# The last attention block turned by TensorE, three outer products by row halves, and the rows after them in a new order

## The chip, the cores and the metric

The kernel runs on one core of one Trainium2 chip. All data is float32. The metric is the device time of one execution in microseconds (us); the median of 3 runs of the kernel before is 1077.04 us (1076.51 to 1078.44). The engines are TensorE (PE: matmuls and 128x128 transposes), VectorE (DVE), ScalarE (ACT), GpSimd (POOL) and SyncE (SP, which only issues transfers). ACT and POOL issue transfers too, each in its own order.

## What is computed

Input x is 1024 x 512. The reference, cut to what matters:

```python
# attention: 32 heads of 128, 8 key/value heads
q = (h @ w_q).reshape(B, S, 8, 4, 128); k = h @ w_k; v = h @ w_v
scores = einsum('bqhgd,bkhd->bhgqk', q, k) * 128 ** -0.5
probs = softmax(where(causal, scores, -inf))
attn = einsum('bhgqk,bkhd->bqhgd', probs, v)
attn_ref = attn.reshape(B, S, 4096) @ w_o
# FFN: a dense layer plus 8 low-rank experts of rank 16
base_out = x @ base_W.T + base_b
probs = softmax(x @ router_W.T + router_b)          # 15 logits
topk_p, topk_i = top_k(probs, 8)
w = sum over k of topk_p * onehot(expert_map[topk_i])
lora = ((x @ A) * w) @ B * 2.0
ffn_ref = base_out + lora
# the whole
x = x + layernorm(attn_ref(layernorm(x)))
x = x + layernorm(ffn_ref(layernorm(x)))
```

## The kernel before

**Rows and groups.** The 1024 rows are 8 blocks t of 128 rows. The 32 heads are 8 groups g of 4 heads, one group to a key/value head. A block of a group is worked in four score tiles j of 32 rows by 4 heads, which fill 128 partitions. Blocks are taken in units (0,1), (2,3), (4), (5), (6), (7) within each group.

**A score tile** (`scores`, from L569) goes through a chain: PE scores, DVE mask and maximum (L587), ACT exp and sum (L602), DVE reciprocal (L610), ACT product with it (L611), and DVE's 32x32 stream transpose into tile T (L618). The rest of p's last 128 columns is cleared by POOL (L567). After the last tile of a unit, `to_keys` (L628) issues 16 transfers K<-T, which bring the transposed 32x32 squares into rows of keys: on SP; in the last group also on POOL for block 6, and on SP, ACT and POOL in turn for block 7. Only then can PE form the block's weighted values (`weighted_values`, L645; `attend` does it for a unit, in that unit's K). Unit i - 2 is attended while unit i's scores are formed, mixed with "fill": other products (q, k, v of the next group, and in the last group the first three steps of the output projection). `cut` divides fill by shares among units and score tiles; `weave` mixes two lists by their cost. In the last group results go into the PSUM banks `last`.

**The output projection** is a 4096-term product. Attention output and w_o are taken in an outer scheme of seven products (Strassen-Winograd), each of which is done in an inner one of seven. Its step (n, gc, r) is outer product n, chunk gc of two heads groups (0 to 3), and row half r, or None for both. A whole step is 28 matmuls, a half step 14. To feed it, ACT copies a block's values into the pair tile `at` (two blocks side by side), DVE forms four outer sums in `pair_sums` (L671), and POOL stores the tile in memory, `attn_d` (`pair_store`, L682; seven parts, 896 KB). `fetch_a` loads a step's operand again and `sums_a` (L768) has DVE form its inner sums; `fetch_w` and `sums_w` (L785) do the same for w_o, on SP and POOL. `merge_inner` (L852) and `merge_outer` (L879) add the products up, from PSUM into `acc`, whose slices are row blocks. Even row blocks are complete after outer product n=4, odd ones after n=6.

**The FFN** for row block t: `ffn_norms` (L924: both layernorms around the first residual, in steps run one by one by `go`), `ffn_router` (L977: PE turns h, `ptx_h`, ACT copies it into hT, PE forms logits and low-rank values `pl`, then DVE, ACT and POOL form routing weights and `hw`), `ffn_out` (L1026: PE's dense products `pf`, `ptw` turns hw, ACT copies it into hwT, PE adds the experts, DVE and POOL finish with the second layernorm), and `ffn_store`. In the program order written out after L1306, steps 0 to 10 are placed by hand around the last blocks; from step 11 on `whole_step` runs each with its loads and sums (`begin_step`, L1354, which forms the sums of step k + 2 ahead). FIRST = 28 is the first half step: outer product 6 is done by halves, r = 0 first (rows 1 and 3, called c and d), then r = 1 (rows 5 and 7, e and f). Rows 0, 2, 4 and 6 of the FFN are woven with these eight half steps; `NORMS` says in which half step which row advances by a norm's step. Rows c to f follow in the tail.

Engines execute their instructions in program order, so a waiting instruction holds up all that stands behind it on its engine.

Of the kernel before, what the change touches and what calls it, by code (L numbers as in the profile page):

```python
# [15 lines left out]
P = 128  # L16
# [6 lines left out]
def kernel(  # L23
# [82 lines left out]
    for k in range(NCH):  # L106
        halves = 2 if k == NCH - 1 else 1
        names = [f"attn_d{k}_{r}" for r in range(halves)]
        shape = [7, GC, P, NT * P // halves]
        attn_d.append([dram.tile(shape, F32, tag=name, name=name) for name in names])  # L110
        wo_d.append(dram.tile([4, GC, P, 2 * hn], F32, tag=f"wo_d{k}", name=f"wo_d{k}"))

# [439 lines left out]
    score_tile = {}  # L552
# [16 lines left out]
    def scores(g, t, j):  # L569

# [36 lines left out]

        def rescale():
            rec = small.tile([P, 1], F32, tag="rec", name=f"rec_{name}")
            keep(nc.vector.reciprocal(rec, total))  # L610
            keep(nc.scalar.mul(p[:, :n], p[:, :n], rec))  # L611
# [14 lines left out]
        score_tile["rescale"], score_tile["finish"] = rescale, finish  # L626

    def to_keys(g, u):  # L628
        size = sum(t + 1 for t in u) * NSUB * P
        src = turned.pop((g, u))[:, :size].rearrange("p (b n) -> p b n", b=NSUB)  # L630
        w = turn_tile("K", g, u)
        dst = w[:, :size].rearrange("p (h n) -> p h n", h=R)
        for t in u:
            keyed[g, t] = turn_view(w, t)
        by = [nc.sync]
        if g == G - 1 and u[0] >= 6:
            by += [nc.gpsimd] if u[0] == 6 else [nc.scalar, nc.gpsimd]
        for h in range(R):
            for b in range(NSUB):
                load(dst[ts(b, SQ), h], src[ts(h, SQ), b], by[(h * NSUB + b) % len(by)])  # L640

    pair_tiles = {}
    last_banks = []

    def weighted_values(g, t):  # L645

        def finish(po):
            if t % 2 == 0:
                pair_tiles[g, t // 2] = act.tile(
                    [P, 7, 2, P], F32, tag="at", name=f"at_{g}_{t // 2}"  # L650
                )
            o = pair_tiles[g, t // 2][:, 2 * (t % 2) : 2 * (t % 2) + 2]
            pinned(nc.scalar.copy(o.rearrange("p a h q -> p (a h q)"), po))
            keyed.pop((g, t))
# [16 lines left out]
    def pair_sums(m):  # L671
        g, u = divmod(m, NT // 2)
        a11, a12, a21, a22, s1, s2, s4 = (pair_tiles[g, u][:, n] for n in range(7))
# [8 lines left out]
    def pair_store(m):  # L682
        g, u = divmod(m, NT // 2)
        at = pair_tiles.pop((g, u)).rearrange("p n h q -> p n (h q)")
# [14 lines left out]
    steps += [(1, 0, None), (1, 1, None), (0, NCH - 1, 1), (1, 2, None), (1, 3, None)]  # L699
    steps += [(n, gc, None) for n in range(2, 6) for gc in range(NCH)]  # L700
    FIRST = len(steps)
    steps += [(6, gc, r) for r in range(2) for gc in range(NCH)]
    HALF = 7 * GC * P
    A_TAGS = ((turn, "T0"), (turn, "K0"), (turn, "K1"), (big, "xnT"), (big, "tx"))
    a_parts, w_parts, ring = {}, {}, {"a": 0}

    def load_a(part, c, by):
        n, gc, r = steps[c]
        size = NT // 2 * P
# [12 lines left out]
    def early_a(c):  # L722

        a, y = divmod((0, 1, 2, 3, 0, 1, 2, 0, 0, 3)[c], 2)
# [19 lines left out]
    def fetch_w(n, gc, by=nc.sync):  # L744
# [3 lines left out]
        places = ("v skv", "wq", "qT", "wo wot", "qT", "wq", "qT", "qT", "wq", "wo wot", "qT", "qT")  # L748
        tags = places[k if (k := n * NCH + gc) < 8 else 8 + k % NCH].split()
        pools = {"qT": (act, 2), "v": (act, 3)}  # L750
        tiles = []
        for tag in tags:
            pool, bufs = pools.get(tag, (wp, 1))
            shape = [P, 2 // len(tags), half]
            tiles.append(pool.tile(shape, F32, tag=tag, name=f"o{tag}_{name}", bufs=bufs))
        w = [tile[:, y] for tile in tiles for y in range(2 // len(tags))]
# [11 lines left out]
    def sums_a(c):  # L768
        a, r = a_parts[c], steps[c][2]
        nr = 2 if r is None else 1  # L770
# [14 lines left out]
    def sums_w(n, gc):  # L785
# [3 lines left out]
        sums = w[1].rearrange("p (n g q) -> p n g q", n=4, g=GC)  # L789
        t1, t2, t3, t4 = (sums[:, y] for y in range(4))  # L790
# [3 lines left out]

    def fetch(c):
        n, gc, r = steps[c]
        fetch_a(c)
        for k in range(1 if r is None else 2):
            if r in (None, 0):
                fetch_w(n, gc + k)  # L800

    def step_sums(c):
        n, gc, r = steps[c]
        sums_a(c)
        if r in (None, 0):
            sums_w(n, gc)
# [45 lines left out]
    def merge_inner(n, r=None):  # L852
        nr = 2 if r is None else 1
        if (n, r) == (0, 1):
            whole = merged[0]
        else:
            rows = 2 if n == 0 else nr
            whole = act.tile([P, 2 * rows, hn], F32, tag="p", name=f"om_{n}_{r}", bufs=3)
        to = whole.rearrange("p (r e) (c q) -> p r e c q", e=2, c=2)
        if n == 0:  # L860
            to = to[:, r : r + 1]
# [17 lines left out]
    def merge_outer(n, r=None):  # L879
# [5 lines left out]
        new = merged[n]  # L885
# [60 lines left out]
    def prepare_ffn():  # L946
        ra = act.tile([P, KC, NR + ER], F32, tag="v", name="ra_sb", bufs=3)
# [17 lines left out]
    mexp = const.tile([P, E, NR], F32, tag="mexp", name="mexp")  # L965

    def prepare_map():
        emap_f = const.tile([P, NR], F32, tag="emap_f", name="emap_f")
        keep(nc.vector.tensor_copy(emap_f, late["map"]))
        for n in range(E):  # L970
            keep(
                nc.vector.tensor_scalar(
                    mexp[:, n, :], emap_f, float(n), SCALING, ALU.is_equal, ALU.mult
# [3 lines left out]
    def ffn_router(t):  # L977
# [19 lines left out]
        def route(pl, ex, total):  # L997
# [13 lines left out]
            keep(nc.vector.tensor_tensor(ws, mexp, every, ALU.mult))  # L1011
            w = small.tile([P, E], F32, tag="w", name=f"w_{t}")
            keep(nc.vector.tensor_reduce(w, ws, AX.X, ALU.add))
            hw = state["hw", t] = wp.tile([P, E, RANK], F32, tag="wk", name=f"hw_{t}")
# [241 lines left out]
    LAST_A_SUMS = ((1, 3), (3, 0), (4, 3), (7, 1))  # L1256
# [4 lines left out]
    for i, (g, u) in enumerate(order):  # L1261
        if u[0] == 0:
            if g < G - 1:
                fill = cut(group_fill(g), FILL if g else FIRST_FILL)
            else:
                first = sum((step_products(k) for k in range(3)), [])
                fill = cut(group_fill(g), (1, 1)) + cut(first, (5, 1.5, 1.3, 1.2))
# [6 lines left out]
        else:  # L1274
            ahead, mine = cut(mine, (1, 1) if u[0] == 5 else (3, 7))
# [3 lines left out]
        for (t, n), part in zip(tiles, parts):  # L1279
            loads(g, t, n)  # L1280
            scores(g, t, n)
            pool_work(g, t, n)
            run(part)
# [23 lines left out]
    finish_scores()  # L1307
# [3 lines left out]
    held.update({t: [] for t in range(NT)})  # L1311
    acc_all = turn.tile([P, NT // 2, 2, H], F32, tag="T1", name="acc")
    acc = [acc_all[:, t // 2, t % 2, :] for t in range(NT)]
    run(attend(NU - 2))
    pair_sums(N // 2 - 2)
    pair_store(N // 2 - 2)
    sums_a(4)
    sums_a(5)
    fetch_a(8)
    sums_w(1, 0)  # L1320
    one_step(3)
    one_step(4)
    sums_a(6)
# [3 lines left out]
    run(attend(NU - 1))  # L1327
    sums_a(8)
    sums_w(1, 1)
    fetch_a(10)  # L1330
    one_step(6)
    pair_sums(N // 2 - 1)
    pair_store(N // 2 - 1)
    fetch_w(1, 2)
    fetch_a(9)
    fetch_a(11)
    one_step(7)
    sums_a(9)
    sums_w(1, 2)
    fetch_w(1, 3)  # L1340
    one_step(8)
    sums_a(10)
    fetch_w(2, 0)
    one_step(9)
    fetch_a(12)
# [3 lines left out]
    fetch_a(13)  # L1349
    fetch_w(2, 1)  # L1350
    sums_a(12)
    sums_w(2, 0)

    def begin_step(k):  # L1354
        if k + 3 < FIRST:
            fetch(k + 3)
        if k >= FIRST - 2 and (k - FIRST) % 2 == 0 and k + 2 < len(steps):
            fetch(k + 2)
        if k + 2 < FIRST:
            step_sums(k + 2)  # L1360
        if k >= FIRST - 1 and k + 1 < len(steps):
            step_sums(k + 1)

    evens = (0, 2, 4, 6)
    NORMS = {-4: (0, 2), -3: (0, 4, 6), -2: (2, 0, 4), -1: (0, 2, 6, 4), 0: (2, 6, 4), 1: (6,)}
    NORMS.update({4: (c, d), 5: (c, d), 6: (c, d), 7: (c, d)})

    def hook(*rows):
        return [(0, lambda: go(*rows))]
# [4 lines left out]
    routers = {t: ffn_router(t) for t in range(NT)}  # L1374
    outs = {t: ffn_out(t) for t in (*evens, c, d, e)}

    def whole_step(k):
        j = k - FIRST
        work = later(lambda: begin_step(k))
        if j in NORMS:  # L1380
            work += hook(*NORMS[j])
        work += step_products(k)
        n, gc, r = steps[k]
        if gc == NCH - 1:
            work += later(lambda: (merge_inner(n, r), merge_outer(n, r)))
        if k == 11:
            work += later(prepare_ffn)
        if k == 14:
            work += later(prepare_map)
        if j == -6:  # L1390
            work += later(lambda: [reload_x(t) for t in evens])
        if j == -5:
            work += later(lambda: [ffn_norms(t, nc.scalar, nc.gpsimd) for t in evens])
        if j == 3:
            work += later(lambda: (reload_x(c, d), ffn_norms(c), ffn_norms(d)))
        return work

    for k in range(11, FIRST):
        run(whole_step(k))

    rows = []
    rows += routers[0][0]
    for n, t in enumerate(evens):
        turn_next = routers[evens[n + 1]][0] if n < 3 else []
        rows += routers[t][1] + hook(t) + outs[t][0] + turn_next + outs[t][2]
        if n:
            rows += hook(evens[n - 1]) + later(lambda t=evens[n - 1]: ffn_store(t))
        rows += outs[t][1] + outs[t][3] + hook(t)
    run(weave(sum((whole_step(k) for k in range(FIRST, len(steps))), []), rows))

    reload_x(e, f)
    ffn_norms(e)
    ffn_norms(f)
    out_c, out_d, out_e = (outs[t] for t in (c, d, e))
    turn_c, prod_c = routers[c]
    turn_d, prod_d = routers[d]
    turn_e, prod_e = routers[e]
    turn_f, prod_f = routers[f]
    go(e, f)
    run(turn_c + prod_c)  # L1420
    go(e, c, evens[-1])
    ffn_store(evens[-1])
    run(out_c[0] + turn_d + out_c[2])
    go(f, e)
    run(prod_d)
    go(f, d, e)
    run(out_c[1] + out_d[0])
    go(f)
    run(out_c[3])
    go(c)  # L1430
    run(out_d[2] + turn_e + out_d[1])
    go(c)
    run(out_d[3] + prod_e)
    go(d, e)
    run(out_e[0] + out_e[2][:1] + turn_f + out_e[2][1:] + prod_f)
# [50 lines left out]
```

## Time and profile before

The profiled execution took 1076.29 us, its span (first to last instruction) is 1074.5 us; the median of the three runs is 1077.04.

| | busy us | share of span | instructions |
|---|---|---|---|
| PE | 1028.9 | 96% | 4722 |
| DVE | 747.9 | 70% | 1786 |
| ACT | 476.4 | 44% | 948 |
| POOL | 366.6 | 34% | 609 |

Stretches of the last third (busy us of each engine, the clock that TensorE was granted as a share of full speed, and the DMA engines' busy share):

| from to, us | what runs | PE | DVE | POOL | PE clock | DMA |
|---|---|---|---|---|---|---|
| 700 to 750 | last group, blocks 0 to 4 | 45.85 | 38.11 | 24.46 | 0.97 | 0.75 |
| 750 to 800 | last group, blocks 5 to 7 | 42.77 | 33.28 | 17.97 | 0.94 | 0.78 |
| 820 to 840 | the very last block's values | 14.42 | 8.57 | 3.69 | 0.83 | 0.89 |
| 840 to 900 | outer products, whole steps | 60.00 | 46.57 | 37.97 | 1.00 | 0.91 |
| 900 to 960 | the same | 60.00 | 49.75 | 38.05 | 1.00 | 0.74 |
| 960 to 980 | product 6 begins | 13.79 | 14.43 | 14.77 | 0.95 | 0.49 |
| 980 to 1000 | product 6 and FFN rows | 20.00 | 11.02 | 4.54 | 0.88 | 0.01 |
| 1000 to 1020 | the same | 16.67 | 14.14 | 2.91 | 0.97 | 0.28 |
| 1020 to 1034 | its end | 13.71 | 8.49 | 4.23 | 0.79 | 0.11 |
| 1034 to 1075 | the tail: rows c to f | 29.48 | 28.06 | 8.96 | 0.94 | 0.12 |

Rows of the profile read as: line of the program, engine, operation, tile written <- tiles read, partitions x elements, and in square brackets how long the engine had been idle before it and what released it. A matmul of float32 shows as two records.

### The profile page before, as it was taken

The page shows a single profiled execution, that of the slowest core. Times are in us where ns is not written, and L with a number is a line of the kernel's source. Part 1 is how long each engine was busy: PE and PEld are TensorE (multiplying, and loading weights), DVE is VectorE, ACT ScalarE, POOL GpSimd, SP SyncE. Part 2 cuts the span into 40 slices and gives each one's busy share as a digit, 9 for nine tenths or more (in the row PEclk, how much of TensorE's full clock was granted, in tenths as well). Part 3 has the DMA queues.
Part 4 walks back from the last instruction along what each step waited for, and adds up shares of the span by engine and source line. Part 5 has one row for each costly group of instructions (what it writes and reads, how often), then busy time and mean ns, then how long its engine had stood idle before and what let it go on. Part 6 is the DMA issues. An engine that isn't in the chain of part 4 may idle for free.

```text
span 1074.5 us, 15038 instructions
## 1 busy us (share of the span) xinstructions
PE 1028.9 (96%) x4722; PEld 726.5 (68%) x4722; DVE 747.9 (70%) x1786; ACT 476.4 (44%) x948; POOL 366.6 (34%) x609
## 2 busy tenths in 40 slices
PE   9999999999999999999999999998887999997878
PEld 7876566667666666666666666665545899996655
DVE  4566667767676767677677767668664599875776
ACT  3556555555655555556555555654452000011112
POOL 2563214211421431142123213235231368664122
PEclk9999999999999999999999999999999999998989
DMA  4157558664765776485667557686786798762211
GB/s 157 31 147 193 143 151 224 160 174 133 214 166 140 204 195 163 129 240 144 160 165 199 155 153 192 170 238 182 206 223 174 269 378 288 268 224 68 69 39 50
DMA packets 80239, 187.45 MB, mean 174 GB/s; under 512 B 16416, under 2 KB 27936, under 8 KB 80160
## 3 DMA queue, kind: packets, MB, share of 16 engines
q1 hardware_dynamic: 61568, 121.08, 41.3%
q0 software_dynamic: 17264, 63.45, 19.0%
q10 hardware_dynamic: 1328, 1.97, 0.7%
q8 instruction: 38, 0.62, 0.2%
q14 instruction: 41, 0.34, 0.1%
HBM read 71.09 MB, written 39.85 MB: 103 GB/s over the span
## 4 chain that ended last, share of the span: by engine, by line
PE 68%; SPq 7%; DVE 6%; DMA 3%; ACT 1%; issue 1%; ACTq 1%; DVEq 0%
PE po L81 17%; PE s L81 15%; PE o L81 14%; PE pq L81 13%; SPq L87 7%; DMA K<-T 3%; PE pf L81 3%; PE last L81 2%; PE pv L81 2%; PE pk L81 1%; DVE T L618 1%; PE pl L81 1%; DVE s L587 1%; ACT p L611 1%; ACTq L87 1%
## 5 line engine op out<-in xcount | busy, mean ns | idle before, releaser
L81 PE MATMUL s<-kT,qT 128*128 128x512 f32 (+15 forms) x768 | 274.6, 467 | 5.5 <-ACT p L602 4.9
L618 DVE STREAM_TRANSPOSE T<-p 128x128 f32<-128x128 f32 (+7 forms) x256 | 198.7, 777 | 112.2 <-ACT p L611 100.7
L602 ACT ACTIVATE p<-s,nmax 128x32 f32<-128x32 f32 (+31 forms) x256 | 179.4, 701 | 194.1 <-DVE nmax L587 186.3
L81 PE MATMUL po<-K,v 128*128 128x512 f32 x504 | 255.7, 597 | 4.1 <-DMA K<-T 4.1
L81 PEld LDWEIGHTS s<-kT,qT 128*128 128x128 f32 x768 | 144.3, 192 | 142.3 <-issue 116.9
L611 ACT ACTIVATE p<-p,rec 128x32 f32<-128x32 f32 (+31 forms) x256 | 188.5, 736 | 116.3 <-DVE rec L610 116.3
L587 DVE CUSTOM_DVE_ANT_0 s<-s,smask 128x32 f32<-128x32 f32 (+31 forms) x256 | 178.7, 698 | 53.8 <-PE s L81 52.6
L567 POOL MEMSET p<- 128x96 f32 (+2 forms) x192 | 29.1, 152 | 400.6 <-DVE T L618 365.2
L81 PEld LDWEIGHTS po<-K,v 128*128 128x128 f32 x504 | 94.0, 191 | 41.9 <-issue 22.7
L782 DVE TENSOR_TENSOR oa<-oa 128x512 f32<-128x512 f32 (+1 forms) x112 | 88.2, 833 | 3.2 <-DMA oa<-attn_d 2.0
L81 PEld LDWEIGHTS o<-oqT,oa 128*128 128x128 f32 x728 | 85.0, 194 | 5.8 <-issue 5.8
L81 PE MATMUL o<-oqT,oa 128*128 128x128 f32 x728 | 85.9, 277 | 0.0
L610 DVE RECIPROCAL rec<-total 128x1 f32<-128x1 f32 x256 | 40.3, 157 | 62.3 <-ACT p L602 59.4
L81 PE MATMUL pq<-xnT,wq 128*128 128x256 f32 x304 | 79.0, 383 | 0.0
L416 DVE TENSOR_TENSOR qT<-pq,qT 128x512 f32<-128x512 f32 x90 | 69.1, 767 | 7.2 <-PE pq L81 7.2
L87 POOL DMA_DIRECT2D attn_d<-at x32 | 30.6, 956 | 126.9 <-DVE rec L610 121.0
L81 PEld LDWEIGHTS pq<-xnT,wq 128*128 128x128 f32 x304 | 55.7, 190 | 19.2 <-issue 13.9
L81 PE MATMUL pq<-tx,sq 128*128 128x256 f32 x240 | 64.7, 379 | 0.0
L792 POOL TENSOR_TENSOR oqT<-oqT 128x256 f32<-128x256 f32 x56 | 47.5, 870 | 43.6 <-DMA oqT<-in_w_o_dram 21.2
L81 PE MATMUL pq<-tx,wq 128*128 128x256 f32 x240 | 61.4, 379 | 0.0
L81 PEld LDWEIGHTS pq<-tx,sq 128*128 128x128 f32 x240 | 44.6, 190 | 24.4 <-issue 19.7
L81 PEld LDWEIGHTS pq<-tx,wq 128*128 128x128 f32 x240 | 45.5, 190 | 16.0 <-issue 9.7
(208 smaller groups left out, 1329.3 us busy)
## 6 DMA issues: line engine op xcount, KB each, us to landing
attn_d<-at POOLq DMA_DIRECT2D x32, 896.0 KB, 6.3
K<-T SPq DMA_DIRECT2D x248, 112.0 KB, 2.3
oa<-attn_d SPq DMA_DIRECT2D x15, 1024.0 KB, 7.5
K<-T SPq DMA_DIRECT2D x118, 128.0 KB, 2.7
K<-T SPq DMA_DIRECT2D x128, 96.0 KB, 2.2
K<-T SPq DMA_DIRECT2D x128, 80.0 KB, 4.4
oa<-attn_d SPq DMA_DIRECT2D x18, 512.0 KB, 6.1
wo<-in_w_o_dram POOLq DMA_DIRECT2D x16, 512.0 KB, 6.3
```

The lines of the kernel that those rows point to most:

```text
L81: keep(nc.tensor.matmul(*args, **kw))
L87: keep(by.dma_start(dst, src))
L416: pinned(nc.vector.tensor_tensor(dst, src, to, ALU.add))
L567: keep(nc.gpsimd.memset(p[:, t * P + (j + 1) * SQ : (t + 1) * P], 0.0))
L587: nc.vector.tensor_tensor_reduce(out=s[:, :n], in0=s[:, :n], in1=smask[:, S - n :], scale=-1.0, scalar=-MASKED, op0=ALU.add, op1=ALU.min, ...
L602: keep(nc.scalar.activation(p[:, :n], s[:, :n], AF.Exp, bias=nmax, scale=-1.0, accum_out=total))
L610: keep(nc.vector.reciprocal(rec, total))
L611: keep(nc.scalar.mul(p[:, :n], p[:, :n], rec))
L618: nc.vector.transpose(turn_view(turned[g, u], t)[:, :, j, :, :].rearrange("p b k q -> p k b q"), p[:, :full].rearrange("p (k b q) -> p k b ...
L782: keep(nc.vector.tensor_tensor(dst, p, q, op))
L792: keep(nc.gpsimd.tensor_tensor(dst, p, q, ALU.subtract))
```

## The change

1. *Very last block (group 7, block 7).* Its score tiles are no longer transposed by DVE and sent through 16 transfers. `turn_on_pe` has TensorE transpose 8 squares of 128 columns of each tile (32 in all) into PSUM; ACT copies the first half and DVE the second into `K_last`. The turn of tile j comes after two pieces of the work that follows a later tile; the last tile's comes after block 6's values. Step 3 stands ahead of the last block's values, and steps 4 to 9 are reordered.
2. *Outer products 4, 5 and 6 by row halves.* FIRST becomes 20, and 24 half steps follow. The loads and sums of weights and operands follow tables (`w_loads`, `w_sums`, `a_loads`), and the tiles for w_o a ring with two more places.
3. *Product 6 without sums at its time.* For odd blocks ACT copies half of po a second time, into a tile `la` (128 x 7 x 128); `pair_sums` forms the inner sums of two such blocks on DVE for every second pair (16 times), and `pair_store` stores them (16 stores of 458 KB, `last_d`) just ahead of that pair's attn_d store. The operands of product 6 are loaded from there (0.92 MB a step, for 0.5 MB), and `sums_a` then only takes views.
4. *Last group.* The first two inner sums are formed at tiles (1,1) and (1,3), not (1,3) and (3,0); fill shares are 6, 2, 1, 0 for 5, 1.5, 1.3, 1.2, and from block 5 on a unit's fill comes ahead of the weighted values.
5. *FFN rows.* Norms of rows 0 and 2 advance in half steps 4 to 7, of 4 and 6 in 8 to 11; rows 0, 2, 4 are woven with half steps 12 to 20, row 6 with 20 to 22, the fronts of c and d with 22 to 24. Row f's norm uses ACT and POOL. The tail has a new order.

Two small tiles also move to other places.

```diff
+        def turn_on_pe(half):
...
+            at = keyed[g, t][:, :, j].rearrange("p h k q -> p k h q")
+            ks = range(NT // 2 * half, NT // 2 * (half + 1))
+            pt = last_banks[2] if j < NSUB - 1 else last_bank(f"pt_{half}")
+            for n, k in enumerate(ks):
+                transpose(pt[:, ts(n, P)], p[:, ts(k, P)], ident)
+            by = nc.vector.tensor_copy if half else nc.scalar.copy
+            pinned(by(at[:, ks[0] : ks[-1] + 1], pt.rearrange("p (k h q) -> p k h q", h=R, q=SQ)))
...
+        if very_last:
+            turns_on_pe.extend([lambda: turn_on_pe(0), lambda: turn_on_pe(1)])
+        else:
+            score_tile["finish"] = finish
...
+            if t % 2:
...
+                two = slice(0, 2) if t % 4 == 1 else slice(2, 4)
+                to = last_tiles[g, t // 4][:, two].rearrange("p h q -> p (h q)")
+                pinned(nc.scalar.copy(to, po[:, 2 * P :]))
...
     def pair_sums(m):
         g, u = divmod(m, NT // 2)
+        sum_halves(*(pair_tiles[g, u][:, n] for n in range(7)))
+        if u % 2:
+            sum_halves(*(last_tiles[g, u // 2][:, n] for n in range(7)))
...
     def pair_store(m):
         g, u = divmod(m, NT // 2)
+        if u % 2:
+            la = last_tiles.pop((g, u // 2)).rearrange("p n q -> p (n q)")
+            load(last_d[g // GC, u // 2][g % GC], la, nc.gpsimd)
...
-    steps += [(1, 0, None), (1, 1, None), (0, NCH - 1, 1), (1, 2, None), (1, 3, None)]
-    steps += [(n, gc, None) for n in range(2, 6) for gc in range(NCH)]
+    steps += [(1, 0, None), (0, NCH - 1, 1), (1, 1, None), (1, 2, None), (1, 3, None)]
+    steps += [(n, gc, None) for n in range(2, 4) for gc in range(NCH)]
     FIRST = len(steps)
-    steps += [(6, gc, r) for r in range(2) for gc in range(NCH)]
+    steps += [(n, gc, r) for n in range(4, 7) for r in range(2) for gc in range(NCH)]
...
     def sums_a(c):
         a, r = a_parts[c], steps[c][2]
+        if steps[c][0] == 6:
+            ops = a.rearrange("p (g n r q) -> p n g r q", g=GC, n=7, r=1)
+            a_parts[c] = [ops[:, n] for n in (0, 1, 6, 3, 4, 5, 2)]
+            return
...
-    LAST_A_SUMS = ((1, 3), (3, 0), (4, 3), (7, 1))
+    LAST_A_SUMS = ((1, 1), (1, 3), (4, 3), (7, 1))
...
-                fill = cut(group_fill(g), (1, 1)) + cut(first, (5, 1.5, 1.3, 1.2))
+                fill = cut(group_fill(g), (1, 1)) + cut(first, (6, 2, 1, 0))
...
-            ahead, mine = cut(mine, (1, 1) if u[0] == 5 else (3, 7))
+            ahead = (1, 0) if g == G - 1 and u[0] > 4 else (1, 1) if u[0] == 5 else (3, 7)
+            ahead, mine = cut(mine, ahead)
...
+            while len(turns_on_pe) > 2:
+                run(part[:2])
+                part = part[2:]
+                turns_on_pe.pop(0)()
             run(part)
...
     run(attend(NU - 2))
     pair_sums(N // 2 - 2)
     pair_store(N // 2 - 2)
+    for turn_part in turns_on_pe:
+        turn_part()
     sums_a(4)
+    run(step_products(3))
     sums_a(5)
+    sums_w(1, 0)
+    merge_inner(0, 0)
+    run(attend(NU - 1))
...
+    times = {4: ((-3, -2), (-2, -1), (-2, -1), (-1, 0)), 5: ((2, 5), (4, 7), (5, 8), (6, 9))}
+    times[6] = ((8, 11), (9, 12), (13, 16), (14, 17))
...
+    a_loads |= {FIRST - 3: FIRST, FIRST - 2: FIRST + 2, FIRST - 1: FIRST + 4}
+    a_loads |= {k - 6: k for k in range(FIRST + 6, len(steps), 2)}
...
-    NORMS = {-4: (0, 2), -3: (0, 4, 6), -2: (2, 0, 4), -1: (0, 2, 6, 4), 0: (2, 6, 4), 1: (6,)}
-    NORMS.update({4: (c, d), 5: (c, d), 6: (c, d), 7: (c, d)})
+    NORMS = {4: (0, 2), 5: (0, 2), 6: (0, 2), 7: (0, 2), 8: (4, 6), 9: (4, 6), 10: (4, 6), 11: (4, 6)}
...
+    run(halves(0, 12))
...
+    run(weave(halves(12, 16), rows))
...
+    run(weave(halves(16, 20), rows))
...
+    run(weave(halves(20, 22), rows))
...
+    run(weave(halves(22, 24), rows))
     reload_x(e, f)
     ffn_norms(e)
-    ffn_norms(f)
+    ffn_norms(f, nc.scalar, nc.gpsimd)
```

## The prediction

> **What bounds the kernel now.** I read the slices of the span first, then TensorE's waits, then its timeline around each wait, then VectorE's and the DMA views of the places that the change touches.
>
> ```profile
> PE   9999999999999999999999999998887999997878
> PEclk9999999999999999999999999999999999998989
> ```
> ```profile
> PE pl L81 <- ACT hT L282: 11.9, 3, 6.2
> PE last L81 <- DMA K<-T: 7.2, 3, 3.7
> PE last L81 <- DMA xnT<-attn_d: 5.6, 1, 5.6
> PE s L81 <- ACT p L602: 4.9, 5, 2.3
> PE pf L81 <- ACT hwT L1039: 4.4, 2, 3.6
> PE po L81 <- DMA K<-T: 4.1, 6, 1.1
> ```
>
> TensorE sets the time: 1028.9 of 1074.5 us busy. Its slices are full until about 720 us; what is missing lies in the last heads group (720 to 835), at 970 and in the tail. The second fence is TensorE's waits (sum in us, times, longest). Apart from 4.1 us in six equal places (groups 1 to 6), all lie behind 720 us. The timeline gives their places (start, duration, idle before):
>
> ```profile
> 744.90 1.13 PE L81 MATMUL s<-kT,qT 128*128 128x512 f32 x2 [2.26 <-ACT p L602]
> 745.87 3.55 PE L81 MATMUL po<-K,v 128*128 128x512 f32 x4
> ...
> 766.49 2.04 PE L81 MATMUL last<-K,v 128*128 128x512 f32 x2 [2.99 <-DMA K<-T]
> ...
> 796.79 1.72 PE L81 MATMUL last<-K,v 128*128 128x512 f32 x2 [3.67 <-DMA K<-T]
> ...
> 830.51 3.75 PE L81 MATMUL last<-K,v 128*128 128x512 f32 x4 [5.58 <-DMA xnT<-attn_d]
> ...
> 979.20 2.28 PE L81 MATMUL pl<-ra_sb,hT 128*128 128x143 f32 x8 [6.21 <-ACT hT L282]
> ...
> 1020.29 2.07 PE L81 MATMUL pf<-bt_bias,hwT 128*128 128x512 f32 x2 [3.63 <-ACT hwT L1039]
> ```
>
> Each idle stretch costs twice: what follows runs at half speed for a while (four po records 3.55 us at 745.87 against 1.88 for four pf of that shape at 1037.26, and the granted clock is 0.79 in 1020 to 1034). The wait at 830.51 is named after a load of xnT, but the instruction reads K of the very last block, whose 16 K<-T transfers were issued just before.
>
> **The change, part by part**, against the span of 1074.5.
>
> 1. *Last block on TensorE.* 16 K<-T transfers go (6 on SP, 5 on ACT, 5 on POOL), and DVE's transposes of that block. Gone: 5.6 us idle, and 2.1 us (its 16 records take 9.17 us, 7.03 at full speed). Added: 32 transposes (four ptx_h take 0.44 us: 3.5 us) and 4+4 copies of 512 columns on ACT and DVE (0.6 us each), behind step 3's 14 products. The last tile's turn still waits for its exp, sum and multiplication on ACT: 1.0. Sum -3.2.
>
> 2. *First outer sums of group 7 moved* from tiles (1,3), (3,0) to (1,1), (1,3). Four sums held DVE for 3.53 and 4.60 us (725.59, 738.77); behind them stood the mask of the next scores, and PE. The idle places at 730 to 745 (0.5, 1.4, 2.3) and the 1.7 of half clock are due to the second; at the earlier tiles, with products to cover them, I keep 0.5 and a first gap of 1.9. Sum -3.5.
>
> 3. *K waits of group 7.* Fill shares (5, 1.5, 1.3, 1.2) become (6, 2, 1, 0) of 9.4 us (42 products of 0.223), and all of a unit's fill comes ahead of its values. Gone: 2.99+1.8 at K_2, 0.57 at K_4 (781.36), 3.67+1.8 at K_5: 10.8. But K_4's rows leave at a T done before the K_2 wait (764.63), and land at 781.3 whatever PE does: of the 4.8 saved at K_2 plus 0.57, fill moved ahead takes 1.05+0.54+0.37, and 3.4 is waited for there, with 1.7 of half clock. That lies between K_5's last T and its use, so 1.0 is left at K_5, 0.3 at K_6. Sum -10.8+6.4 = -4.4.
>
> 4. *FFN rows.* Row 0's transposed h was late at 979.20: its normalisation began after the fifth product and stood among sums. Now all even rows are normalised in half steps 4 to 11 and their products woven from half step 12, some 25 us (8 times 3.1) later than the norms' start. Gone: 6.2+2.8 there (pl 2.28 for 1.12, o 1.71 for 0.89, pf 1.71 for 0.86), and 3.6+2.9 at 1020 (pf 2.07 for 1.02, o 1.91 for 1.05, pl 2.10 for 1.12), since a route has half steps of product beside it. Sum -15.5.
>
> 5. *Products five to seven by halves.* PE's count is unchanged (28 products a whole step, 14 a half). DVE's is not:
>
> ```profile
> 961.32 3.59 DVE L782 TENSOR_TENSOR oa<-oa 128x256 f32<-128x256 f32 x4
> ```
>
> This is a half step's sums with POOL busy beside them (14.77 of 20 us in 960 to 980); four of the same shape with POOL idle take 1.55. The first twelve half steps (products five and six, first half) last 37.5 us. DVE then has 12 such sums, three merges of 2.7 (1.92 at 1004.54, 0.76 behind), four rows of norms of 2.4 (17.7 us in all): 36.3 us at 1.55, 60.9 at 3.6. Between them: whole sums of 512 columns take 975 ns in 845 to 970 and 650 with POOL idle, 1.5 times; by that 2.33 a half step, 45.6 in all, 8.1 over, of which the lead of two half steps covers 6.3. I take 2 (bounds 0 and 17), and 4 for POOL, where the weight sums (0.72 to 1.17 each, four per step) of (5,1) to (5,3) stand behind four x-adds (1.3) and eight powers (0.55): +6 (bounds 0 and 21).
>
> 6. *Front of rows c and d (1 and 3).* Their transposes, now in the last two half steps, wait for DVE's chain behind the seventh product's first merge: 2.3 idle and 1.5 of clock by the rows of 1020; +3.8 (bounds 0 and 4).
>
> 7. *Tail.* From the last product (1033.3) to the end 41.2 us now. Front work of c and d of 4.6 (two ptx_h 0.44, two pl 1.1, pf 1.7) goes ahead of that point; behind it e's and f's chains set the end: last DVE work about 32.4 after it, then 3.75 as now: 36.2. Sum -0.4.
>
> 8. *Seventh product's sums in the attention.* 32 copies on ACT (0.38), 64 sums of 128 columns on DVE (0.29, in 16 places of 1.2 us) and 16 stores of 458 KB issued on POOL (0.96 each). ACT (56%) and DVE (70%) have room in the attention; a hold of 1.2 us is under the smallest that made PE wait (3.53). If that cover were gone, 1.5. The stores are different. The one of pair 3 is issued in unit 4, ahead of the 896 KB of attn_d, while K_2's rows are on their way, and K_2 lands just when PE wants it in groups 1 to 6 (the six waits of 0.4 to 1.1 above). K<-T alone moved this (556 to 560, then 560 to 564, queue, MB and share):
>
> ```profile
> q1 hardware_dynamic: 299, 0.69, 74.6%
> ```
> ```profile
> q0 software_dynamic: 223, 0.88, 66.5%
> q1 hardware_dynamic: 123, 0.30, 35.6%
> ```
>
> Beside a store it moves 0.30 MB in 4 us. 0.458 MB more at 0.88 per 4 us are 2.1 us of company, in which K<-T falls behind by 0.2 MB, 1.2 us. Bounds for seven groups: 0 (the loss falls on rows with time) and 14.6 (2.1 each); taken +7.
>
> *Sum:* -3.2-3.5-4.4-15.5+6+3.8-0.4+7 = -10.2, a span of 1064.3. The run was 1.8 longer than its span (1076.29) and the median is 0.75 above that: 1067.
>
> **Where the skill speaks against this.** Rows first: 2.26 us idle at 744.90 are followed by half speed. The Trainium skill, "TensorE: Matmul & The Clock Gate", section "What's actually happening", throttles only after an idle window of about 3.4 us. By it the 1.7 at K_4 might not come: 1065. The other: sums of one shape took 1.55 or 3.59 us. "SBUF — State Buffer", section "SBUF: two separate sides", says a VectorE operation with two SBUF inputs and a GpSimd operation that reads SBUF lock each other out for whole instructions; so shorter operations pay more often. As an estimate by it, each of four 0.39 us operations waits for half of a 0.92 us one 70% of the time: 2.85 a half step, DVE 8 us late instead of 2, 1073.
>
> **Rivals.**
>
> *A, better:* POOL's and DVE's halves keep their lead and stores fall beside K_2's slack (+6, +3.8, +7 become 2, 1, 3): 1056. For it: DVE is at 49.75 of 60 in 900 to 960 without one PE wait. Against: K_2 has no slack in six groups.
>
> *B, no change:* DVE's half sums take 3.6 each, as at 961.32, and starve PE: +17 for 6, 1078. For it: POOL is at 38 of 60 there. Against: 3.59 stood beside a POOL run of x-adds.
>
> *C, slower:* the stores of last_d in unit 4 push K_2 by more than the threshold of the clock. Seven waits of 2.1, each with 1.7 of half clock (as at 745.87): 26.6 for 7, 1087. It decides from 17/7 = 2.4 us a group. For it: the four transfers beside the store of 560.7 landed in 5.5 us, those before it in 2.3. Against: the attn_d store already falls there, and only the later half of K_2's 16 transfers.
>
> *D, not what it says:* the last block's copies or K_7's products still wait, since its last T is replaced by PE work behind the same chain; 7.7 comes back: 1075.
>
> **How the numbers follow.** Forecast 0.44, A 0.20, B 0.13, C 0.16, D 0.07. The forecast's own range, terms 5, 6 and 8 combined as squares: 1057 to 1076. To leave 2 in 10 out, it is carried to 1052 (A with its terms near nothing) and 1081 (B, and a part of C). A measurement tells 0.2%, 2.2 us. Faster: forecast 0.44, A 0.20, half of D (0.035), a third of B (0.045): 0.72. Same: the other half of D and half of B: 0.10. Slower: C and the rest of B: 0.18.
>
> **What would show it.** Right: no idle in front of the last K,v products; none of 6 us before pl; waits for K<-T in groups 1 to 6 grown from 0.7 to near 2 us each. A: those waits still under 1. B: DVE full and PE idle with oa as releaser in the five half products. C: waits over 2.3 with slow po behind. D: a wait of last for ACT or DVE copies of over 3 us. The forecast is wrong if the tail from the last product is longer than 41 us, or if halves leave PE waiting for POOL's weight sums over 6 us.

## The result, and the profile after

The changed kernel takes 1111.83 us (median of four runs, 1103.14 to 1114.86) against 1077.2 for the kernel before: ratio 1.0307, interval 1.0243 to 1.0371. It is slower by some 33 us, where 10 us faster was forecast. The profiled run took 1109.05 us, its span is 1107.1.

TensorE's waits, by what they ended on (sum in us, times, longest), in the changed kernel:

```profile
PE po L81 <- DMA K<-T: 16.2, 10, 2.3
PE ptx_h L84 <- DVE h L259: 8.4, 2, 4.7
PE last L81 <- DMA K<-T: 6.8, 3, 3.0
PE pl L81 <- ACT hT L287: 4.3, 1, 4.3
...
PE last L84 <- ACT K_last L625: 3.6, 3, 1.8
...
PE o L81 <- POOL oat L839: 2.0, 2, 1.6
PE po L81 <- DVE nmax L591: 2.0, 3, 0.7
PE o L81 <- DVE oa L830: 1.6, 1, 1.6
PE o L81 <- POOL owot L839: 1.6, 2, 1.4
```

The wait for the very last block (5.6 before) is gone and the longest wait for hT has shrunk from 6.2 to 4.3. But po's waits for K<-T, 4.1 before, are 16.2, and there are new ones: for the copies of the turned block, for POOL's and DVE's sums in the half steps, and for DVE's h. The span is best cut at places where both kernels run the same instruction (its start in us on TensorE's timeline):

| place | before | after | difference | added since the place above |
|---|---|---|---|---|
| first score of group 0 | 39.1 | 40.3 | +1.2 | +1.2 |
| third score tile of block 2, group 7 | 730.4 | 754.6 | +24.2 | +23.0 |
| what follows the very last block's values | 839.5 | 856.9 | +17.3 | -6.9 |
| what follows the last outer product | 1034.9 | 1070.2 | +35.3 | +18.0 |
| end of the span | 1074.5 | 1107.1 | +32.6 | -2.7 |

Two half steps (4 and 5, 6.3 us) are moved past the third place, and the fronts of rows 1 and 3 (4.8) ahead of the fourth. Without these the stages differ by +23.0, -0.6, +6.9 and +2.1. Of the 23.0, 1.8 lie in the first blocks of group 7 and 21.2 in groups 0 to 6. So two thirds of the loss lie where the change only adds the seventh product's copies, sums and stores. There, in windows between the first two places (stretch, its length, then PE, PEld, DVE, ACT and POOL busy, clock, DMA share, GB/s), before and after:

```profile
39.09:730.35 691.26, 684.60 (x2586) 448.80 (x2586) 486.06 (x1189) 388.31 (x766) 203.26 (x384) 1.00 0.65 172
```
```profile
40.29:754.58 714.29, 692.17 (x2586) 450.67 (x2586) 498.61 (x1245) 396.23 (x793) 211.32 (x397) 0.99 0.65 176
```

The same 2586 matmul records: idle time rose from 6.7 to 22.1 us, busy time from 684.6 to 692.2. TensorE's timeline gives the parts. The six waits at K_2 (groups 1 to 6) are 12.7 us, for 4.0 before. Seven waits of 0.5 to 1.5 us stand at K_5, one in each of groups 0 to 6, 5.5 in all (the rows name K<-T or DVE's nmax); before there were none. Behind three of the six waits at K_2 the granted clock is 0.50 for 3.4 us, which costs 1.7 each.

### The profile page after: what moved, and what is told of

The parts are those of the page before. It is cut to its first block, busy times and chain, and to the rows that moved or that the text cites. A ratio compares the mean times of both kernels' runs of the same rounds, so it can differ in the third digit from the quotient of the medians.

```text
span 1107.1 us, 15178 instructions
## 1 busy us (share of the span) xinstructions
PE 1041.4 (94%) x4754; PEld 733.5 (66%) x4754; DVE 755.2 (68%) x1864; ACT 489.4 (44%) x988; POOL 376.1 (34%) x621
## 3 DMA queue, kind: packets, MB, share of 16 engines
q1 hardware_dynamic: 62912, 123.44, 40.3%
## 5 line engine op out<-in xcount | busy, mean ns | idle before, releaser
L81 PE MATMUL po<-K,v 128*128 128x512 f32 x504 | 257.4, 600 | 18.2 <-DMA K<-T 16.2
L637 DVE STREAM_TRANSPOSE T<-p 128x128 f32<-128x128 f32 (+7 forms) x252 | 193.7, 769 | 115.5 <-ACT p L630 102.0
L830 DVE TENSOR_TENSOR oa<-oa 128x256 f32<-128x256 f32 (+1 forms) x112 | 83.3, 790 | 10.0 <-DMA oa<-attn_d 8.7
L81 PEld LDWEIGHTS o<-oqT,oa 128*128 128x128 f32 x504 | 58.4, 192 | 3.8 <-issue 3.8
L81 PE MATMUL o<-oqT,oa 128*128 128x128 f32 x504 | 59.2, 275 | 0.0
L715 DVE TENSOR_TENSOR at<-at 128x256 f32<-128x256 f32 x128 | 47.9, 416 | 4.7 <-ACT at L676 3.6
L897 ACT COPY om<-o 128x256 f32<-128x256 f32 (+1 forms) x10 | 4.3, 430 | 105.5 <-PE o L81 105.5
```

Of the source, the lines that this page charges most:

```text
L81: keep(nc.tensor.matmul(*args, **kw))
L637: nc.vector.transpose(turn_view(turned[g, u], t)[:, :, j, :, :].rearrange("p b k q -> p k b q"), p[:, :full].rearrange("p (k b q) -> p k b ...
L715: keep(nc.vector.tensor_tensor(dst, p, q, op))
L830: keep(nc.vector.tensor_tensor(dst, p, q, op))
```

## The experiments

**First question: is it the seventh product's part, and which piece of it?** *e1_own_sums* is the changed kernel without that part; *e2_part3* is the kernel before with that part alone; *e3_stores* and *e4_la_only* put its stores alone, and its copies and sums alone, into the kernel before.

e1_own_sums, against the changed kernel:

```diff
-                pinned(nc.scalar.copy(to, po[:, 2 * P :]))
...
-            sum_halves(*(last_tiles[g, u // 2][:, n] for n in range(7)))
...
-            load(last_d[g // GC, u // 2][g % GC], la, nc.gpsimd)
...
-            load(to, last_d[gc, r].rearrange("g p n -> p g n"), by)
...
-        if steps[c][0] == 6:
...
```

> The changed kernel without the seventh product's sums in the attention: no second copies, no la sums, no last_d stores; product 6 loads 0.5 MB from attn_d and DVE forms its sums at its time, as in the kernel before. Theory (the loss of some 22 us in groups 1 to 6 comes from this part): waits of po for K<-T fall from 16.2 to about 4, the attention ends 20 us or more sooner, the time is 1084 to 1092. Rival (the other parts of the change cost the time, through the runs' spread): still over 1100.

e2_part3 adds these same lines to the kernel before, and moves a small table (`mexp`) to make room.

> The kernel before with this part alone (copies, sums and stores in the attention, product 6 from last_d; a small mask table moved to make room). Theory: the same 20 to 24 us in the attention, less nothing behind it, since its outer stage waited for no sums of product 6: 1095 to 1102. Rival (the part costs only together with the others): within 5 us of 1077.

e3_stores, against the kernel before, in `pair_store`:

```diff
+        if u % 2:
+            la = pair_tiles[g, u].rearrange("p n h q -> p (n h q)")[:, : 7 * P]
+            load(last_d[g // GC, u // 2][g % GC], la, nc.gpsimd)
```

> The kernel before with 16 more stores of 448 KB alone, from the pair tile, just ahead of the same attn_d stores; what they store is read by nobody. Traffic theory: nearly the whole loss, 1092 to 1100, with po waiting for K<-T some 16 us. Engine theory (ACT's copies and DVE's sums make the T tiles late): at most 1080.

e4_la_only adds the copies and `sum_halves` of e2_part3, without store and load. The table is moved here too; no run moves it alone.

> The kernel before with ACT's 32 second copies and DVE's 64 sums alone, their result read by nobody, no stores. Traffic theory: at most 1080. Engine theory: 1092 to 1100, and T tiles some 2 us later against the scores in unit 4.

| run | median, us | ratio to before | interval | PE waits po <- K<-T |
|---|---|---|---|---|
| e1_own_sums | 1088.07 | 1.0111 | 1.0072 to 1.0149 | 3.4 |
| e2_part3 | 1104.1 | 1.0260 | 1.0223 to 1.0296 | 17.4 |
| e3_stores | 1090.27 | 1.0136 | 1.0103 to 1.0170 | 11.2 |
| e4_la_only | 1085.08 | 1.0084 | 1.0054 to 1.0114 | 4.7 |

By the ratios the part costs 28 us in the kernel before and 21 in the changed one. Neither the traffic theory nor the engine theory has it all: stores alone cost 15 us, copies and sums alone 9, and the two together a little more than their sum. In e3_stores the wait at K_2 in groups 1 to 6 is 1.6 to 2.7 us long (two of the six rows name ACT's p, and are not in the table's 11.2); this is TensorE's timeline at two of them and, in the middle, at a second place, at K_5 two units further on, where the kernel before had no wait:

```profile
480.69 1.10 PE L81 MATMUL po<-K,v 128*128 128x512 f32 x2 [1.79 <-DMA K<-T]
...
609.44 1.10 PE L81 MATMUL po<-K,v 128*128 128x512 f32 x2 [0.66 <-DVE T L623]
...
679.12 1.10 PE L81 MATMUL po<-K,v 128*128 128x512 f32 x2 [2.15 <-DMA K<-T]
```

In e4_la_only the waits are others, short ones of the scores for ACT, about once per group:

```profile
428.93 0.54 PE L81 MATMUL s<-kT,qT 128*128 128x160 f32 x2 [0.63 <-ACT p L602]
...
527.58 0.54 PE L81 MATMUL s<-kT,qT 128*128 128x160 f32 x2 [0.55 <-ACT p L602]
```

These waits are 8.9 us in all for 4.9 before. That is 4.0 of the 8.2 us by which the span grew; where the rest comes from is only partly seen (waits for K are 1.2 longer).

**Is it the traffic or its place?** *e9_stores_moved* issues as many stores of the same size where TensorE waits for no K.

```diff
+            if (t, n) in ((2, 2), (7, 2)):
+                load(last_d[g // GC, t // 4][g % GC], smask[:, : 7 * P], nc.gpsimd)
```

> The kernel before with 16 more stores of 448 KB as in e3_stores (1.014 of before), but issued at score tiles (2,2) and (7,2), where PE waits for no K, instead of ahead of the attn_d stores at (4,2) and (6,2); they store a constant mask that nobody reads. If the place decides (K_2's and K_5's transfers have no slack in units 4 and 6): within 4 us of before. If 7.3 MB more of traffic costs wherever it falls: 10 us slower or more.

Measured: 1075.51 us, ratio 0.9992 (0.9975 to 1.0009). The same 16 stores cost 15 us at (4,2) and (6,2) and nothing at (2,2) and (7,2). So it is the place and not the amount, with one reservation: these stores read a constant tile that is ready at once. One new wait, 3.7 us for K_6 in group 7, is made up by shorter ones after it. The DMA view of eight microseconds from the issue on in group 5, after, then before (queue, packets, MB, share; q0 carries the stores, q1 K<-T):

```profile
q0 software_dynamic: 383, 1.63, 58.4%
q1 hardware_dynamic: 300, 0.72, 39.2%
...
K<-T SPq DMA_DIRECT2D x7, 112.0 KB, 5.0
```
```profile
q0 software_dynamic: 375, 1.43, 53.3%
q1 hardware_dynamic: 310, 0.74, 41.7%
...
K<-T SPq DMA_DIRECT2D x7, 112.0 KB, 4.6
```

The stores' queue already filled this stretch (its next store, wo_d, moved back); 0.2 MB more of it delays K<-T a little each time. From SP's first issue of K_2 to TensorE's use of it are 16.2 us before (553.12 to 569.36) and 17.8 after (566.29 to 584.04). The last of K_2's 16 transfers lands 0.35 us ahead of that use both times.

**Copies or sums?** *e15_copies_only* is e4_la_only without DVE's sums.

```diff
-            sum_halves(*(last_tiles[g, u // 2][:, n] for n in range(7)))
```

> e4_la_only (1.008 of before) without DVE's 64 sums: ACT's 32 second copies of po alone. If DVE's hold of 1 us in front of the next tile's mask makes the loss of e4: within 3 us of before. If ACT's copies in front of the next exp make it: 6 to 9 us slower.

Measured: 1081.94 us, ratio 1.0040 (1.0023 to 1.0057), 4 us slower: between the two expectations. About half of the 9 us of e4_la_only comes with the copies, half with the sums. The short waits of the scores, one per group in e4_la_only, are mostly gone here, so the sums have a part in them.

**Second question: the last group.** *e5_pe_turn* is the kernel before with the last block turned by TensorE, *e6_group7* with the last group's order alone, *e12_sums_only* with only its two sums moved, *e8_both* has e5 and e6 together.

```diff
# e6_group7; e12_sums_only has the first line alone
-    LAST_A_SUMS = ((1, 3), (3, 0), (4, 3), (7, 1))
+    LAST_A_SUMS = ((1, 1), (1, 3), (4, 3), (7, 1))
...
-                fill = cut(group_fill(g), (1, 1)) + cut(first, (5, 1.5, 1.3, 1.2))
+                fill = cut(group_fill(g), (1, 1)) + cut(first, (6, 2, 1, 0))
...
-            ahead, mine = cut(mine, (1, 1) if u[0] == 5 else (3, 7))
+            ahead = (1, 0) if g == G - 1 and u[0] > 4 else (1, 1) if u[0] == 5 else (3, 7)
+            ahead, mine = cut(mine, ahead)
# e5_pe_turn: turn_on_pe as in the change, and at the end
     pair_store(N // 2 - 2)
+    for turn_part in turns_on_pe:
+        turn_part()
     sums_a(4)
```

> The kernel before with the very last block turned by TensorE alone; its turns stand ahead of steps 3, 4 and 5, so their copies have 9 us of products behind them. Theory by the changed kernel's trace (its own price): 5.0 us of transposes and up to 5.6 us of waits for the single bank and the copies against 5.6 idle and 2.1 of slow clock that go: within 3 us of the kernel before, 1074 to 1080. The prediction's step 1: 3 us faster.

> The kernel before with the last group's sums at (1,1), (1,3), its fill shares 6, 2, 1, 0 and all fill ahead of the values. Prediction's steps 2 and 3: 8 us faster. Rival (the waits for K only move along the group, and the sums hold DVE elsewhere): within 2 us of the kernel before.

> The kernel before with the last group's first two sums at (1,1) and (1,3), the fill as before. Prediction's step 2: 3.5 us faster. If the fill shares and the fill put ahead of the values make e6_group7's 4.7 us: within 1 us of before.

> e5_pe_turn and e6_group7 together, with the outer stage, the FFN rows and product 6 of the kernel before. If both gain as predicted: 1066. If the K waits only move along the group: 1073 to 1077. It is the version that could beat both.

| run | median, us | ratio to before | interval |
|---|---|---|---|
| e5_pe_turn | 1077.81 | 1.0012 | 0.9994 to 1.0030 |
| e6_group7 | 1072.70 | 0.9957 | 0.9941 to 0.9973 |
| e12_sums_only | 1074.78 | 0.9986 | 0.9971 to 1.0001 |
| e8_both | 1075.33 | 0.9985 | 0.9970 to 0.9999 |

The order of the last group gains 4.6 us, of which 1.5 may be the sums' place. Turning the block on TensorE gains nothing, and on top of the new order (e8_both against e6_group7) it gives 3 us back. Its timeline in e5_pe_turn shows why:

```profile
808.00 0.66 PE L84 MATMUL last<-ident,p 128*128 128x128 f32 x4 [0.66 <-ACT K_last L621]
812.22 0.65 PE L84 MATMUL last<-ident,p 128*128 128x128 f32 x4 [0.81 <-ACT p L626]
813.87 0.66 PE L84 MATMUL last<-ident,p 128*128 128x128 f32 x4 [1.00 <-ACT K_last L621]
...
819.40 0.66 PE L84 MATMUL last<-ident,p 128*128 128x128 f32 x4 [0.78 <-ACT K_last L621]
820.91 7.97 PE L81 MATMUL last<-K,v 128*128 128x512 f32 x14 [0.85 <-DVE K_last L621]
```

For the first three tiles both halves go through one PSUM bank, so the second four transposes wait for the copy of the first, and block 6's values, which use that bank too, wait for the last copy. That is 3.3 of the 4.1 us of idle here (4.5 of 5.6 in the changed kernel); the rest is a wait for ACT's p. The 32 transposes take 4.0 us from start to next start. Together that stands in place of 5.6 idle and 2.1 of slow clock: no gain.

**Third question: the half steps.** Four kernels start from e1_own_sums. *e7_norms_later* puts the last norm step of rows 4 and 6 from half step 11 into 13, *e11_pool_early* POOL's weight sums of n = 5 a half step earlier, *e10_front_late* the fronts of rows 1 and 3 behind the last product; *e14_no_sums5* is e10 without DVE's sums for n = 5.

```diff
# e7_norms_later
-    ..., 10: (4, 6), 11: (4, 6)}
+    ..., 10: (4, 6), 13: (4, 6)}
# e11_pool_early
-    5: ((2, 5), (4, 7), (5, 8), (6, 9))}
+    5: ((2, 5), (4, 6), (5, 7), (6, 8))}
# e10_front_late
-    run(weave(halves(22, 24), rows))
+    run(weave(halves(22, 24), hook(6) + store(6)))
...
     go(e)
+    run(rows)
# e14_no_sums5, against e10_front_late, in sums_a
+        if steps[c][0] == 5:
+            a_parts[c] = (a11, a12, a12, a22, a11, a22, a21)
+            return
```

> The changed kernel without the seventh product's sums in the attention (as e1_own_sums, 1088), and the last step of the norms of rows 4 and 6 in half step 13 instead of 11, so that ACT's two activations for h of these rows stand behind row 0's copy into hT. Theory (pl of row 0 waits because ACT stands in order behind those, which wait for DVE's late shift): the wait of pl for hT falls from 4.3 to under 1.5, 4 to 6 us faster than e1_own_sums, 1082 to 1084. Rival (row 0's chain itself is late): the wait stays at 4.

> e1_own_sums with POOL's weight sums of product 5's steps 1 to 3 a half step (3.1 us) earlier. Theory (POOL is late behind the x-adds and powers of the norms): the waits of o for POOL's owot and oat (3.6 us) and their half clock go: 3 to 5 us faster than e1. Rival (DVE's sums are the later of the two at the same places, or POOL's loads are): under 1.5 us.

> The changed kernel without the seventh product's sums in the attention (e1_own_sums, 1088), with the fronts of rows 1 and 3 behind the last product instead of in its last two half steps. Theory (PE meets these fronts too early: ptx_h waits 6.6 us for DVE's h, with half clock after it): that wait goes and the tail grows by the front's 4.8 us of work at most: 3 to 6 us faster than e1. Rival (what is waited for there is waited for in the tail in any case): within 2 us of e1.

> e10_front_late without DVE's inner sums of product 6 of 7 (n = 5), whose eight half steps then use the loaded parts as they are: 32 DVE operations left out. Theory (with halves, DVE and POOL together are late, each waiting for the other's place in memory): the waits of o for DVE's oa and for POOL's owot and oat in product n = 5 (5.2 us) and the 4.3 of pl fall by half or more, 5 to 9 us faster than e10_front_late. Rival (POOL alone is late): waits for oa go, those for POOL stay, under 3 us.

| run | median, us | ratio to before | interval |
|---|---|---|---|
| e1_own_sums | 1088.07 | 1.0111 | 1.0072 to 1.0149 |
| e7_norms_later | 1086.79 | 1.0093 | 1.0072 to 1.0114 |
| e11_pool_early | 1088.93 | 1.0108 | 1.0084 to 1.0131 |
| e10_front_late | 1080.79 | 1.0033 | 1.0014 to 1.0052 |
| e14_no_sums5 | 1072.77 | 0.9950 | 0.9932 to 0.9967 |

e7_norms_later: the wait of pl is gone, as the in-order theory has it, but 2.9 us come up at the next product of that row (pf for hwT), and the time hardly moves. e11_pool_early: the waits for POOL's owot and oat go and DVE's take their place. Waits of o in e1_own_sums, then in e11_pool_early:

```profile
PE o L81 <- POOL oat L818: 2.0, 2, 1.6
PE o L81 <- DVE oa L809: 1.6, 1, 1.6
PE o L81 <- POOL owot L818: 1.6, 2, 1.4
```
```profile
PE o L81 <- DVE oa L809: 4.5, 3, 3.7
```

e10_front_late: 8 us less than e1_own_sums by the ratios, more than expected; ptx_h's waits for DVE's h fall from 11.4 to 2.6 us. e14_no_sums5: another 9 us less. The wait of pl for row 0's hT falls from 4.3 to 2.0, and with DVE's sums the waits for POOL go as well:

```profile
PE o L81 <- POOL owot L821: 0.4, 2, 0.2
...
PE o L81 <- POOL oat L821: 0.2, 1, 0.2
```

So DVE is what is late in the half steps, and POOL with it: its weight sums for n = 5 stand behind x-adds and powers of the norms that wait for DVE.

**The version that beats both.** *e13_row0* is e6_group7 with a later norm step for rows 2, 4 and 6.

```diff
-    ..., -1: (0, 2, 6, 4), 0: (2, 6, 4), 1: (6,)}
+    ..., -1: (0, 2, 6, 4), 1: (2, 6, 4), 2: (6,)}
```

> e6_group7 (0.9957 of before) with the norm steps of rows 2, 6, 4 that the kernel before takes ahead of half step 0 of product 6 taken ahead of half step 1, and row 6's next ahead of 2, so that ACT's h of rows 2 and 4 stand behind row 0's copy into hT. In-order theory: the 6.2 us wait of pl at 979 and the half clock behind it go, 6 to 9 us faster than e6. Rival (DVE, not ACT's order, sets the pace there, and the wait moves to the next row's product): within 2 us of e6.

Measured: 1070.48 us, ratio 0.9938 (0.9917 to 0.9959): 6.7 us faster than the kernel before, and the fastest of all kernels here. Against e6_group7 it is 2 us, which the intervals don't tell from nothing. The 6.2 us of pl are gone; row 2's turn now waits:

```profile
978.91 1.12 PE L84 MATMUL ptx_h<-ident,h 128*128 128x128 f32 x4 [5.16 <-ACT h L258]
```

ACT's h there waited for DVE's shift_h, and that is the rival's case: DVE sets the pace, and the wait moves.

## Why the prediction was wrong

*Step 8 (the seventh product's part)* is the step that failed: +7 was taken, with 0 to 14.6 as bounds for the stores and 1.5 for the rest; it is +28 on the kernel before (e2_part3), where stores alone make 15 and copies and sums alone 9. Its mechanism at K_2 was right and well sized: in e3_stores the six waits of groups 1 to 6 average 1.9 us for 0.7 before, 1.3 more each, for 1.2 forecast. In the changed kernel they average 2.1. The signs named for the forecast all came (no idle ahead of the very last block's values, none of 6 us before pl, waits for K<-T near 2 us), and neither sign of its being wrong did: they watched what had been priced. What was missed:
- The second store, at (6,2), was not weighed against the keys of block 5. New waits stand there, two units behind those at K_2: 2.2 us in e3_stores, 5.5 in the changed kernel.
- "ACT and DVE have room in the attention" was a share over the stage, and the test used (a hold of 3.5 us made PE wait, so 1.2 would not) took the smallest hold seen for the smallest that matters. e4_la_only shows waits of 0.4 to 1.1 us of the scores for ACT, and 9 us of time; in e15_copies_only the 0.38 us copies on ACT alone cost 4.
- The slow clock behind the waits at K_2 had no term: three stretches of 1.7 us, 5.1 of the 7.6 us more busy time for the same matmuls.

*Rival C* named the place, the queue and the sign, and had the nearest time (1087). Its price for the slow clock, 1.7 after each wait of 2.1, came for three of the five waits of over 2.1 us at K_2 in the changed kernel (2.26, 2.31 and 2.31, not 2.19 and 2.22). It, too, had nothing for K_5, for the copies and for the sums.

*Step 1 (last block):* -3.2 forecast, +1.3 measured (-0.6 to +3.2). The old wait of 5.6 did go. But the transposes took 4.0 for 3.5, and 1.0 was allowed for waits of the turns, where they came to 4.1 to 5.6, most of it from one PSUM bank in two uses. It is rival D's mechanism, in a milder form.

*Steps 2 and 3 (last group):* -7.9 forecast, -4.6 measured in e6_group7. The direction and the passing of the wait from K_2 to K_4 were right: in e6_group7 it is 3.66 us for 3.4, and K_5 kept 0.81 for 1.0. The gap in front of the third tile of block 2, taken as 1.9, is 2.54 there, and the scores wait 1.7 us for ACT in units 6 and 7, where they had no wait. Against this the wait for the very last block fell from 5.6 to 3.7, which neither step had. In the changed kernel the gap is 2.75, with half clock behind it, and K_5 kept 2.54.

*Steps 4, 5 and 6 (rows and half steps):* -15.5, +6 and +3.8, so -5.7, were forecast; the stage is 6.9 longer. Step 4 took the waits for hT and hwT to go because the norms begin 25 us earlier than the products. They begin earlier, but on a DVE that e14_no_sums5 shows to be the bound: 4.3 us stayed at pl. This chain shows it in the changed kernel (start, duration):

```profile
993.95 2.08 DVE L830 TENSOR_TENSOR oa<-oa 128x256 f32<-128x256 f32 x4
...
995.95 0.32 DVE L262 TENSOR_SCALAR shift_h<-mv_h,rstd_h 128x1 f32<-128x1 f32 x2
996.19 1.52 ACT L263 ACTIVATE h<-acc,shift_h,rstd_h 128x512 f32<-128x512 f32 x2 [6.75 <-DVE shift_h L262]
...
997.87 0.58 ACT L287 COPY hT<-ptx_h 128x512 f32<-128x512 f32 x1
```

Row 0's hT, whose transposes were done at 993.3, stands on ACT behind h of rows 4 and 6, and those behind a half step's sums on DVE. Step 6 (fronts of rows 1 and 3, +3.8, bounds 0 and 4) cost 8.4 us by e1_own_sums against e10_front_late, the tail included: the bounds were those of one wait of 2.3, and the one in the last half steps is 6.6 in e1_own_sums (3.7 in the changed kernel), with a longer wait for row e's h in the tail beside it. For step 5's +6 (bounds 0 and 21) there are 5.2 us of waits for oa, owot and oat in the changed kernel, and the slow clock. Leaving out DVE's sums of n = 5 gains 9 us (e14_no_sums5), but part of that is pl's wait, so the runs do not part step 5 from step 4. Another 2.6 us of waits stand in the whole steps, at 908 to 911 us (for osq's load and POOL's owk); no step had them.

*Step 7 (tail):* -0.4 forecast; the tail is 2.7 shorter, with 4.8 of its work moved out: +2.1. The forecast began the old tail at 1033.3, but the last outer product ends at about 1034.9, so its own sum was 1.6 too low. The waits for e's and f's h, 4.7 and 2.9, were not in it.

The Trainium skill's lock between VectorE and GpSimd ("SBUF — State Buffer", section "SBUF: two separate sides") spoke against the half steps, and the price by it, 1073 for 1067, had the right sign. These runs do not separate it from plain order: with DVE's sums left out (e14_no_sums5), POOL's subtractions for owot and oat in 930 to 970 us take 726 ns, where in e10_front_late they take 752 to 946 on average, while the waits of TensorE for them went nearly to nothing.

What stays open: how ACT's copies cost 4 us in e15_copies_only (its waits are few, and 3.6 us of the loss lie in waits for K in the last group), how copies and sums with the stores make the waits at K_5 longer than the stores alone do, and which part of the last 2 us of the tail is order and which DVE.

## What to carry to other kernels

Before a transfer is added, look up which transfers run beside it, and which of those land just when they are needed: the same 7 MB cost 15 us at two places of a group and nothing at two others. A busy share over a stage is no room: where each tile passes a chain over four engines, small operations put into it are paid for, and only a wait that the trace shows to end elsewhere is a cover. When a wait is removed, ask whether the engine behind it, here DVE, has time at all; otherwise it comes back at the next instruction.

## What was not expected of the hardware

The prediction had every long idle stretch cost twice, once as idle time and once by the slow clock behind it. The slow clock does not follow from the length of a wait alone. Behind the wait of 2.31 us at 584.04 in the changed kernel the first records of po still take 1.10, their value after a wait of 0.53 us before. The records from 585.0 on are slow: the next two of po take 1.91, for 1.02 before. The granted clock (0.50 in the third row here, a window of 3.41 us) falls there and not at the end of the wait:

```profile
584.04 1.10 PE L81 MATMUL po<-K,v 128*128 128x512 f32 x2 [2.31 <-DMA K<-T]
...
585.78 1.91 PE L81 MATMUL po<-K,v 128*128 128x512 f32 x2
```
```profile
585.00:588.41 3.41, 3.41 (x8) 1.99 (x7) 1.30 (x2) 0.36 (x1) 2.73 (x4) 0.50 1.00 289
```

The other half-speed stretches behind K_2 begin at 383.6 and 687.4, that is 59 and 30 times 3.413 us away. Divide the time into steps of 3.413 us through these beginnings. Then the three waits that cost clock (2.26 us up to 382.47, and 2.31 up to 584.04 and 686.66) each lie within one step, the one just ahead of the slow stretch. The two that cost none (2.19 up to 183.33, 2.22 up to 484.11) lie across the end of a step, at 182.2 and 482.6, with at most 1.5 us on either side. So it is idle time within a step that counts here, not the length of a wait. The 2.26 us at 744.90 before did cost clock: half speed begins at 745.9 there, and the step ahead of that, from 742.5, holds the whole wait.

The Trainium skill ("TensorE: Matmul & The Clock Gate", section "What's actually happening") has a free-running window of about 3.4 us; these rows agree with that. It lets the clock fall after an idle window; here about 2.3 us of idle within one were enough.
